# Gathering rows for the second step during the first, and computing root steps on GpSimd, in a two-layer graph kernel

## The chip, the cores and the metric

The kernel runs on one core of a Trainium2 chip. Times are device microseconds of one execution. The engines are called by the profile's names: PE (TensorE matmul; PEld its weight load), DVE (VectorE), ACT (ScalarE), POOL (GpSimd) and SP (SyncE, which here only issues DMAs). Each engine works through its own instruction queue in order. "SPq" and "POOLq" are rows for DMAs issued on SP and POOL.

## The reference, cut to what matters

There are N = 2708 nodes with D = 256 features. `adj` has about 0.3% nonzeros and a full diagonal.

```
# layer 0
x = LN(x + relu(concat(x, adj @ x) @ weight + bias))
# layer 1: X = x
R = (adj + I) / rowsum(adj + I)
Xf = X; Xa = X; Z = 0
for n in 0, 1:
    A  = top_p_attention(Xa, W1, W2, W3)   # softmax of (N, N) logits, cut at mass 0.9, renormalized
    Xf = R @ Xf
    Xa = A @ Xa
    Z += Xf @ U1[n].T + Xa @ U2[n].T
out = LN(X + Z)                            # (h - mean) / sqrt(var + 1e-5)
```

As R is sparse, R @ Xf is computed on gathered rows: for each block of 128 rows at most 7 x 128 columns of `adj` hold a nonzero outside the block's own columns.

## The kernel before, in words

The nodes form 22 row blocks of 128 (NB = 22); the last one (EDGE) has 20 rows. The order of the instructions on every engine is the order in which the program issues them.

**Layer 0** takes the time up to about 280 us: the product adj @ x (line 257), the layer norm. In the meantime POOL and DVE find the columns that each block needs (class with `take` and `end`, up to line 348). `end` (lines 324 to 348) is a chain: DVE counts, POOL writes and reads the list through DRAM with DMAs, DVE turns the counts into positions (line 339), and seven more DMAs of POOL follow. It is issued for a first part of the blocks before step 1 and for the rest at block 8 of step 1, slot 2.

**Step 1** (the loop at line 896) is the first attention, one row block after the other, in six slots g = 0 to 5 for each block (NG = 6). A slot holds transposes of the weights (line 527, copied by ACT in line 530), products (line 564), logits of a later block, and DVE's search for the cut, which has one 3 us operation for each block (line 635). Beside this, in dictionary `at`, POOL's `adj_gather(m)` (lines 360 to 371) collects the adjacency of block m: SP loads the own columns (line 364), POOL turns the names of the block before into row numbers (`name_y`, line 358), gathers 7 groups of columns with an indirect DMA each (line 367), and adds the identity to the own columns (line 369, which waits for SP's load). Four and five slots later SP stores the result to DRAM (`adj_store`, lines 373 to 381). At the end of each block SP also stores za (line 703), the running sum Z, from a tile of two buffers that DVE fills in line 702. `step1_out` returns the three steps that follow a block; the last three run after the loop.

After the loop eleven calls of `ya_pair` (line 662) project the attention result, two row blocks at a time, into the tile ya (22 blocks of 256 columns), copied from PSUM by ACT in line 675. Until then ya is not in use.

**The R product** runs in units, one matmul (line 749) for each gathered column group of a block and one for its own block: 8 units a block, 22 blocks, two passes (s = 0 and 1), 352 units. Pass 0 multiplies rows of yf_d (X U1[1]), whose result is added to v_d; pass 1 multiplies v_d. `r_load(s, m)` (line 729) issues the loads of a block as the block before it begins: the adjacency (448 KB and 64 KB, by SP), seven indirect DMAs of POOL which gather 128 rows of 1 KB each (`y_load`, line 719) into one of two buffers yg, and the own rows (line 735, SP). The first two gathers of pass 0 are issued in step 1, at block 20, slots 2 and 5 (`y_at`).

**Step 2** (the loop at line 1271) is the second attention, in 24 periods of six slots. Period `per` transposes and multiplies row block per - 2, computes logits and exponentials of block per + 2 and steps the search of the blocks between; DVE's mask (line 1087) ends each period, and 22 of them lie in the trace. `r_units(n)` spreads the R units over the slots. By period, the numbers of units are:

| period | 0, 1 | 2 to 9 | 10 | 11 to 21 |
|---|---|---|---|---|
| units each | 8 | 18 | 0 | 16 |

16 units (`first`) are computed ahead of period 0. The first 22 blocks (176 units) are pass 0, whose last unit lies in period 9; pass 1 lies in periods 11 to 21.

**The finals.** When both products of a block have arrived (`arrive`, line 785, one addition on DVE), the block takes two layer norms (with `x1b` between them), in `final_slot(i)`, called in each slot i: slot 2 loads x1b, slot 3 takes statistics on DVE, slot 5 takes `roots` (line 1216: ACT's Sqrt of the variances of up to four blocks), slot 0 of the next period takes `over` (line 1219: DVE's reciprocal and the negated mean over the root) and applies the norms (ACT's line 1191, then POOL's lines 1206 and 1207), and slot 1 stores. ACT's Sqrt and its Exp (line 844) lie in different function tables, and changing takes an ACT_TABLE_LOAD. After the loop a tail (line 1323 on) finishes the last blocks with three more root steps, one after the other.

Of the kernel before, what the change touches and what calls it, by code (L numbers as in the profile page):

```python
# [9 lines left out]
FP = mybir.dt.float32  # L10
I32 = mybir.dt.int32
AF = mybir.ActivationFunctionType
ALU = mybir.AluOpType
# [24 lines left out]
KS = 7  # L38
CAP = 160
ML = 16  # L40
CW, CC = 128, 7


# [8 lines left out]
@with_exitstack  # L52
def gnn_two_layer_kernel(ctx: ExitStack, tc: tile.TileContext, N, xT_d, x_d, adj_d, w0_d, b0_d,
                         w1_d, w2_d, w3_d, u1_d, u2_d, g_d, b_d, out_d):

    nc = tc.nc
    D = x_d.shape[1]
    DA = w1_d.shape[1]  # L80
    NB = (N + P - 1) // P
    DC = D // P
    assert N % 2 == 0 and NB % 2 == 0 and N * 2.0 ** -15 < 0.09 and DC == 2 and DA == 64
    assert SEG * (NS - 1) + 8 <= N <= SEG * NS == SEG2 * NS2 and N >= SEG2 * (NS2 - 1) + 8
    assert NB == 3 * KS + 1 and CW == P and CAP % 8 == 0 and N < NB * P
# [20 lines left out]
    c.v_d = dram.tile([P, NB, D], FP, name="v_d")  # L106
    c.own_d = dram.tile([NB, P, P], FP, name="own_d")
# [41 lines left out]
def fast_path(ctx, tc, c, flags, fint, xT_d, x_d, w0_d, b0_d, w1_d, w2_d, w3_d, u1_d, u2_d, g_d, b_d):  # L149
# [561 lines left out]
    arrived, loads, held = {}, {}, {}  # L711
    later = [[], []]
    ready = []

    def y_load(s, m):
        y = yg[:, m % 2]
        rows_d = (c.yf_d, c.v_d)[s].rearrange("p k d -> (p k) d")
        for i in range(CC):
            nc.gpsimd.indirect_dma_start(out=y[:CW, i, :], out_offset=None, in_=rows_d,  # L719
                                         in_offset=bass.IndirectOffsetOnAxis(ap=ix[:CW, m, i:i + 1], axis=0))  # L720
        y_in[s, m] = y

    def a_load(m):
# [39 lines left out]
    def za_load(m):  # L763


        if loads.get(m):
            loads[m] = 2
            return None
        loads[m] = 1
        base = work.tile([P, D], FP, tag="in", name="base", bufs=3)  # L770
        nc.sync.dma_start(out=base[:rows(m)], in_=za_d[m * P:m * P + rows(m), :])
        return base

    def r_out(s, m, acc, base):
        p = rows(m)
        if s == 0:
            nc.vector.scalar_tensor_tensor(base[:p], acc[:p, :D], rinv[:p, m:m + 1], base[:p],
                                           op0=ALU.mult, op1=ALU.add)
            nc.sync.dma_start(out=c.v_d[:p, m, :], in_=base[:p])
            if m == NB - 1:  # L780
                r_load(1, 0)
        else:
            arrive(m, base, acc, rinv[:p, m:m + 1])

    def arrive(m, base, part, scale):

        p = rows(m)
        if base is None:
            h = base = held.pop(m)
        else:  # L790
            h = work.tile([P, D], FP, tag="h", name="h", bufs=5)
# [98 lines left out]

    at = {(m // 2, 3 * (m % 2) + 1): m for m in range(4)}
    at.update({(m - 2, 3): m for m in range(4, NB)})
    y_at = {(NB - 2, 2): 0, (NB - 2, 5): 1}
    stores = []
    blocks = {}
    for t in range(NB):
# [6 lines left out]
        for g in range(NG):  # L903
# [23 lines left out]
            if (t, g) in at:  # L927
                adj_gather(at[t, g])
                stores += [(NG * t + g + i, at[t, g], i - 4) for i in (4, 5)]
            if (t, g) in y_at:  # L930
                name_y()
                y_load(0, y_at[t, g])
            if (t, g) == (NB - 1, 2):
                a_load(0)
        if t == EDGE:
# [4 lines left out]
    assert not stores and not staged and not to_turn  # L940
    r_load(0, 0)
    for f in ends:
        ya_pair()
# [219 lines left out]
    sds = small.tile([P, 8], FP, tag="sds", name="sds", bufs=1)  # L1163
    nbs = small.tile([P, 8], FP, tag="nbs", name="nbs", bufs=1)
    nc.gpsimd.memset(mvs, 1.0)

    class Final:

# [45 lines left out]
            nc.sync.dma_start(out=out_d[t * P:t * P + p, :], in_=self.h[:p])  # L1214

    def roots(a, b):
        nc.scalar.activation(sds[:, a:b], mvs[:, a:b, 1], AF.Sqrt, bias=c.eps, scale=1.0)

    def over(a, b):
        nc.vector.reciprocal(sds[:, a:b], sds[:, a:b])  # L1220
        nc.vector.scalar_tensor_tensor(nbs[:, a:b], mvs[:, a:b, 0], -1.0, sds[:, a:b], op0=ALU.mult, op1=ALU.mult)

    def final_slot(i):


        if i == 2:
            while ready and len(new) < 2:
                new.append(Final(*ready.pop(0)))
                new[-1].load()
        if i == 1:  # L1230
            while done:
                done.pop().store()
        n = len(new) + len(finals)
        if i == 3:
            for k, f in enumerate(new + finals):
                f.stats(k)
        if i == 5 and n:
            roots(0, n)
        if i == 0 and n:
            over(0, n)  # L1240
            for f in finals:
                f.end()
            for f in new:
                f.middle()
            done[:] = finals
            finals[:] = new
            new.clear()

    accs = {}


    each = NB * (CC + 1)
    first = 2 * (CC + 1)
    units = {0: CC + 1, 1: CC + 1}
    rest = each - first - sum(units.values())
    units.update({p: rest * (p - 1) // 8 - rest * (p - 2) // 8 for p in range(2, 10)})
    units.update({p: each * (p - 10) // 11 - each * (p - 11) // 11 for p in range(11, 22)})
    assert first + sum(units.values()) == 2 * each


# [10 lines left out]
    for per in range(NB + 2):  # L1271
        if per == NB + 1:
            tail.append(True)
        n_r = units.get(per, 0)
        b_act = blocks.get(per + 1)
        t_mul = per - 2 if per > 1 else None
        if t_mul is not None:
# [3 lines left out]
            b_exp = blocks[per + 2] = Block(per + 2)  # L1281
        vector = vector_slots(blocks.get(per), blocks.get(per - 1), begin_search(b_exp) if b_exp else None)
        for g in range(NG):
            n = n_r * (g + 1) // NG - n_r * g // NG
            now = later.pop(0)
            later.append([])
            if g == 0:
# [23 lines left out]
                    try_act(b_act, k, part)  # L1311
            next(vector)
            if g == 0:
                final_slot(0)
                if t_mul:
                    t = t_mul - 1
                    base = za_load(t)
                    later[0].append(lambda t=t, base=base: arrive(t, base, accs.pop(t), ras.pop(t)[:rows(t)]))
            for f in now:
                f()  # L1320
            if g and (per < NB + 1 or g < NG - 1):
                final_slot(g)
    t = EDGE
    base = za_load(t)
    last = Final(t, None)
    last.load()
    for f in later[0] + later[1]:
# [18 lines left out]
    arrive(t, base, accs.pop(t), ras.pop(t)[:rows(t)])  # L1346
    _, last.h = ready.pop()
    n = len(new) + len(finals)
    last.stats(n)
# [380 lines left out]
```

## Time and profile before

| quantity | us |
|---|---|
| median of 3 runs | 1323.01 |
| their range | 1322.98 to 1323.81 |
| profiled execution, its time | 1323.33 |
| its span in the trace | 1321.6 |
| PE busy in the span | 1237.4 |
| DVE busy | 1002.0 |
| ACT busy | 753.3 |
| POOL busy | 634.7 |
| layer 0 and preparation | up to 348 |
| step 1 | 348 to 730 |
| projections `ya_pair` | 730 to 754 |
| step 2 | 754 to 1321.6 |

The profiled execution is one of the runs, and its time stands 1.7 us above its span in the trace. Busy time counts instructions, not the gaps between them, nor register, semaphore and DMA-issuing instructions. In the group lines of a profile a row reads: line, engine, operation, output<-input, count | busy us, mean ns of one | idle time of the engine just before them, and what ended most of it. In a windows view each row is a stretch A:B, its length, the busy time of each engine with its number of instructions, the granted PE clock (1.00 is full), the busy share of the DMA engines and GB/s. In a timeline a row is start, duration, engine, line, operation, and in brackets the idle time before it with its releaser. In a waits view a row is the waiting instruction, what released it, and us in total, times, longest.

### The profile page before, as it was taken

What the parts mean: (1) busy time and instruction counts of PE and PEld (TensorE: products, weight loads), DVE (VectorE), ACT (ScalarE), POOL (GpSimd) and SP (SyncE); (2) the same over time, 40 slices, a digit from 0 to 9 for tenths busy, and PEclk for the clock granted to TensorE, in tenths of its full rate; (3) what the DMA queues carried; (4) which work ended last, traced back from release to release, by engine and by line L of the source; (5) the groups of instructions that cost most, each with busy time, mean ns of one, the idle gap of its engine ahead of it and who ended that gap; (6) DMA issues with size and microseconds to landing.
All of it is one profiled execution on the core that took longest, in us unless ns stands there. A gap on an engine that the chain in (4) does not pass through costs nothing.

```text
span 1321.6 us, 18910 instructions
## 1 busy us (share of the span) xinstructions
PE 1237.4 (94%) x5764; PEld 894.5 (68%) x5764; DVE 1002.0 (76%) x3420; ACT 753.3 (57%) x1338; POOL 634.7 (48%) x594
## 2 busy tenths in 40 slices
PE   8999999979899999999999969999999989998985
PEld 6877877833477777777775647777756766666763
DVE  2545555865999998877751399898897999899996
ACT  2010111025465556566564498878888899989931
POOL 1000000005275532677554187887847767787850
PEclk9999999989899999999998979999999999999998
DMA  7455544523222210223232155556545445544541
GB/s 191 163 173 168 167 153 142 171 67 123 92 77 82 70 62 10 76 91 99 76 77 86 55 172 179 177 178 184 172 118 159 148 128 166 173 148 146 166 108 38
DMA packets 101994, 166.28 MB, mean 126 GB/s; under 512 B 17394, under 2 KB 74358, under 8 KB 101882
## 3 DMA queue, kind: packets, MB, share of 16 engines
q1 hardware_dynamic: 75596, 108.91, 25.4%
q0 software_dynamic: 20544, 51.17, 14.1%
q10 hardware_dynamic: 5742, 4.89, 1.3%
q8 instruction: 48, 0.79, 0.2%
q14 instruction: 64, 0.52, 0.1%
HBM read 130.87 MB, written 34.03 MB: 125 GB/s over the span
## 4 chain that ended last, share of the span: by engine, by line
PE 70%; ACT 15%; DVE 11%; issue 3%; DMA 0%; ACTq 0%; DVEq 0%
PE acc L564 23%; PE acc L257 16%; PE lg L507 8%; PE tr L527 6%; PE misc L749 5%; ACT e L965 4%; ACT e L844 3%; ACT e L968 2%; DVE e L1087 2%; PE acc L651 2%; PE acc L462 2%; PE misc L426 2%; PE misc L392 2%; ACT e L848 2%; PE acc L672 2%
## 5 line engine op out<-in xcount | busy, mean ns | idle before, releaser
L530 ACT COPY wT<-tr 128x512 f32<-128x512 f32 (+2 forms) x258 | 131.8, 518 | 217.6 <-PE tr L527 215.9
L564 PE MATMUL acc<-ya,wT 128*128 128x256 f32 (+1 forms) x924 | 234.9, 394 | 11.4 <-ACT wT L530 11.0
L564 PE MATMUL acc<-x,wT 128*128 128x256 f32 (+1 forms) x924 | 230.5, 388 | 0.0
L719 POOL DMA_INDIRECT yg<-v_d,ix x154 | 195.0, 1266 | 64.6 <-issue 25.1
L564 PEld LDWEIGHTS acc<-ya,wT 128*128 128x128 f32 (+1 forms) x924 | 171.4, 194 | 66.0 <-issue 23.1
L719 POOL DMA_INDIRECT yg<-yf_d,ix x154 | 190.7, 1238 | 48.3 <-issue 24.3
L564 PEld LDWEIGHTS acc<-x,wT 128*128 128x128 f32 (+1 forms) x924 | 165.2, 189 | 71.0 <-issue 37.3
L257 PE MATMUL acc<-y,adj_t 128*128 128x257 f32 (+1 forms) x924 | 208.4, 381 | 0.0
L257 PEld LDWEIGHTS acc<-y,adj_t 128*128 128x128 f32 (+1 forms) x924 | 171.8, 189 | 32.7 <-issue 8.9
L367 POOL DMA_INDIRECT adj_t<-in_adj,ix x154 | 165.6, 1076 | 51.8 <-issue 41.7
L749 PE MATMUL misc<-yg,adj_t 128*128 128x256 f32 (+1 forms) x704 | 180.6, 392 | 5.9 <-DMA yg<-yf_d,ix 4.3
L507 PE MATMUL lg<-k,q 64*128 64x512 f32 (+3 forms) x528 | 152.4, 605 | 29.7 <-ACT e L848 22.3
L749 PEld LDWEIGHTS misc<-yg,adj_t 128*128 128x128 f32 (+1 forms) x704 | 125.2, 190 | 54.3 <-issue 23.1
L527 PE MATMUL tr<-ident,e 128*128 128x128 f32 (+2 forms) x946 | 147.9, 275 | 2.5 <-DVE e L1087 2.5
L527 PEld LDWEIGHTS tr<-ident,e 128*128 128x128 f32 (+2 forms) x946 | 114.1, 140 | 41.9 <-issue 18.8
L334 POOL DMA_DIRECT2D part_d<-e x1 | 0.6, 573 | 285.3 <-DVE e L333 285.3
L439 ACT COPY x1T<-tr 128x256 f32<-128x256 f32 (+1 forms) x22 | 8.0, 364 | 186.7 <-PE tr L438 186.7
L965 ACT ACTIVATE e<-e,st 128x2708 f32<-128x2708 f32 (+1 forms) x43 | 113.5, 2640 | 0.1
L968 ACT ACTIVATE e<-e,st 128x2708 f32<-128x2708 f32 (+1 forms) x42 | 111.0, 2642 | 0.1
L570 DVE MAX8 cand<-e 128x8 f32<-128x170 f32 (+1 forms) x352 | 87.2, 317 | 27.4 <-ACT e L514 27.4
L1029 DVE MAX8 cand<-w 128x8 f32<-128x136 f32 (+1 forms) x440 | 106.1, 285 | 0.0
L507 PEld LDWEIGHTS lg<-k,q 64*128 64x128 f32 (+1 forms) x528 | 39.5, 184 | 63.5 <-ACT e L848 30.1
(239 smaller groups left out, 1780.8 us busy)
## 6 DMA issues: line engine op xcount, KB each, us to landing
adj_t<-in_adj SPq DMA_DIRECT2D x44, 704.0 KB
adj_t<-adjc_d SPq DMA_DIRECT2D x44, 448.0 KB
adjc_d<-adj_t SPq DMA_DIRECT2D x22, 256.0 KB
base<-za_d SPq DMA_DIRECT2D x41, 128.0 KB
adjc_d<-adj_t SPq DMA_DIRECT2D x22, 192.0 KB
xt<-in_x ACTq DMA_DIRECT2D x21, 128.0 KB
x_d<-x SPq DMA_DIRECT2D x21, 128.0 KB
x1b_d<-xb SPq DMA_DIRECT2D x21, 128.0 KB
```

The lines of the kernel that those rows point to most:

```text
L257: nc.tensor.matmul(acc[:p, :n], lhsT=halves[k // KH][:kw, k % KH, :p], rhs=y[:kw, k, :n], start=k == 0, stop=stop and k == NB - 1)
L367: nc.gpsimd.indirect_dma_start(out=a[:CW, i, :], out_offset=None, in_=adj_rows, in_offset=bass.IndirectOffsetOnAxis(ap=ix[:CW, m, i:i + 1] ...
L507: nc.tensor.matmul(lg[:p, h, :b - a], lhsT=q[o, t * P:t * P + p], rhs=keys[s][o, i, :b - a], start=True, stop=True)
L527: nc.tensor.transpose(tr[:kw, k % 4, :p], e[:p, k * P:k * P + kw], ident[:p, :p])
L530: nc.scalar.copy(wT[:, :full, :p], tr[:, :full, :p])
L564: nc.tensor.matmul(acc[:p, :D], lhsT=wT[:kw, k % 4, :p], rhs=y[:kw, k, :], start=k == 0, stop=k == NB - 1)
L570: nc.vector.max(dst[:p, i * 8:(i + 1) * 8], src[:p, i * step:i * step + w])
L719: nc.gpsimd.indirect_dma_start(out=y[:CW, i, :], out_offset=None, in_=rows_d, in_offset=bass.IndirectOffsetOnAxis(ap=ix[:CW, m, i:i + 1], ...
L749: nc.tensor.matmul(acc[:p, :D], lhsT=a[:kw, k, :p], rhs=y[:kw, k, :], start=k == 0, stop=k == CC)
L965: nc.scalar.activation(scr[:b.p, :N], e, AF.Relu, bias=b.nz, scale=b.l[k], accum_out=b.relu)
L968: nc.scalar.activation(scr[:b.p, :N], e, AF.Sign, bias=b.nz, scale=b.l[k], accum_out=b.sign)
L1029: nc.vector.max(b.cand[:p, 8 * i:8 * i + 8], low[:p, SEG2 * i:SEG2 * (i + 1)])
```

## The change

1. In step 1, `y_at` now has 14 entries (NY = 14). At slot 0 of blocks 2, 3, 5, 6, 7, 8, 10, 11, 12, 14, 15, 16, 17 and 19 POOL gathers the y rows of row blocks 0 to 13 into a third of the tile ya (blocks of 7 columns, m modulo 3), and seven slots later SP stores them to a new DRAM tile yg_d (896 KB each). In step 2, `y_load(0, m)` of these 14 blocks is one SP load of 896 KB in place of seven indirect DMAs of POOL. The first two of these loads are issued at the last block of step 1, slots 0 and 3. The other eight blocks of pass 0, and all of pass 1, are gathered in step 2 as before.
2. The R units are spread in another way:

| period | 0, 1 | 2 to 8 | 9 | 10 to 21 |
|---|---|---|---|---|
| units each | 24 | 16 | 8, in slots 3 to 5 | 14 |

Pass 0 now ends with period 8, and pass 1 begins in period 9.

3. `roots` is two operations of POOL, an addition of epsilon and a power of -0.5 (by a tile that holds -0.5), so that `over` no longer takes a reciprocal. In `final_slot`, statistics and roots lie in slot 5, `over` and the norms in slot 2 of the next period, stores and loads in slot 3. The tail uses the same `roots`. Slot 5 of the last period takes statistics too, but no roots.
4. `arrive` finds its base tile in a dictionary (bookkeeping).

In the issue order of the changed program POOL has 304 rows for 248, ACT 25 fewer, DVE 16 fewer, SP 26 more and PE 3 more. On SP, the store of stage 13 stands behind the first half of the adjacency store of block 21. The ACT copy of the fourth `ya_pair` (columns 6 and 7 of ya) waits for that store.

```diff
+    def y_gather(s, m, y):
         rows_d = (c.yf_d, c.v_d)[s].rearrange("p k d -> (p k) d")
         for i in range(CC):
             nc.gpsimd.indirect_dma_start(out=y[:CW, i, :], out_offset=None, in_=rows_d,
                                          in_offset=bass.IndirectOffsetOnAxis(ap=ix[:CW, m, i:i + 1], axis=0))
+    def y_stage(m):
+        k = CC * (m % 3)
+        return ya[:, k:k + CC, :]
+    def y_store(m):
+        nc.sync.dma_start(out=c.yg_d[m], in_=y_stage(m)[:CW].rearrange("p c d -> p (c d)"))
+    def y_load(s, m):
+        y = yg[:, m % 2]
+        if s == 0 and m < NY:
+            nc.sync.dma_start(out=y[:CW, :CC, :].rearrange("p c d -> p (c d)"), in_=c.yg_d[m])
+        else:
+            y_gather(s, m, y)
         y_in[s, m] = y
...
-    y_at = {(NB - 2, 2): 0, (NB - 2, 5): 1}
+    y_at = {(2 + m + (2 * m + 3) // 7, 0): m for m in range(NY)}
+    y_stores = []
...
+            if y_stores and y_stores[0][0] <= NG * t + g:
+                y_store(y_stores.pop(0)[1])
             if (t, g) in y_at:
-                name_y()
-                y_load(0, y_at[t, g])
+                y_gather(0, y_at[t, g], y_stage(y_at[t, g]))
+                y_stores.append((NG * t + g + 7, y_at[t, g]))
+            if t == EDGE and g in (0, 3):
+                y_load(0, g // 3)
...
+    name_y()
...
     def roots(a, b):
-        nc.scalar.activation(sds[:, a:b], mvs[:, a:b, 1], AF.Sqrt, bias=c.eps, scale=1.0)
+        nc.gpsimd.tensor_scalar(sds[:, a:b], mvs[:, a:b, 1], LN_EPS, None, op0=ALU.add)
+        nc.gpsimd.tensor_tensor(sds[:, a:b], sds[:, a:b], power[:, a:b], op=ALU.pow)
     def over(a, b):
-        nc.vector.reciprocal(sds[:, a:b], sds[:, a:b])
...
     def final_slot(i):
-        if i == 2:
-            while ready and len(new) < 2:
-                new.append(Final(*ready.pop(0)))
-                new[-1].load()
-        if i == 1:
-            while done:
-                done.pop().store()
         n = len(new) + len(finals)
-        if i == 3:
-            for k, f in enumerate(new + finals):
-                f.stats(k)
-        if i == 5 and n:
-            roots(0, n)
-        if i == 0 and n:
+        if i == 2 and n:
             over(0, n)
...
+        if i == 3:
+            while done:
+                done.pop().store()
+            while ready and len(new) < 2:
+                new.append(Final(*ready.pop(0)))
+                new[-1].load()
+        if i == 5:
+            for k, f in enumerate(new + finals):
+                f.stats(k)
+            if n and not tail:
+                roots(0, n)
...
-    units = {0: CC + 1, 1: CC + 1}
+    units = {0: 3 * (CC + 1), 1: 3 * (CC + 1)}
...
-    units.update({p: rest * (p - 1) // 8 - rest * (p - 2) // 8 for p in range(2, 10)})
-    units.update({p: each * (p - 10) // 11 - each * (p - 11) // 11 for p in range(11, 22)})
+    units.update({p: rest * (p - 1) // 7 - rest * (p - 2) // 7 for p in range(2, 9)})
+    TURN = 9
+    units[TURN] = CC + 1
+    rest = each - units[TURN]
+    units.update({p: rest * (p - TURN) // 12 - rest * (p - TURN - 1) // 12 for p in range(TURN + 1, 22)})
+    def r_share(per, g):
+        late = NG // 2 if per == TURN else 0
+        upto = [units.get(per, 0) * max(0, i - late) // (NG - late) for i in (g, g + 1)]
+        return upto[1] - upto[0]
...
             if g == 0:
-                final_slot(0)
...
-            if g and (per < NB + 1 or g < NG - 1):
+            if g:
                 final_slot(g)
```

More of the change, by code (lines that the diff above doesn't have):

```diff
@@ L40 @@
 ML = 16
+NY = 14
 CW, CC = 128, 7
@@ L106, in gnn_two_layer_kernel @@
     c.v_d = dram.tile([P, NB, D], FP, name="v_d")
+    c.yg_d = dram.tile([NY, CW, CC * D], FP, name="yg_d")
     c.own_d = dram.tile([NB, P, P], FP, name="own_d")
@@ L710, in fast_path @@
     r_in, a_in, y_in = {}, {}, {}
-    arrived, loads, held = {}, {}, {}
+    arrived, loads, held, bases = {}, {}, {}, {}
     later = [[], []]
     ready = []
-    def y_load(s, m):
-        y = yg[:, m % 2]
+    def y_gather(s, m, y):
         rows_d = (c.yf_d, c.v_d)[s].rearrange("p k d -> (p k) d")
@@ L769, in za_load @@
         loads[m] = 1
-        base = work.tile([P, D], FP, tag="in", name="base", bufs=3)
+        bases[m] = base = work.tile([P, D], FP, tag="in", name="base", bufs=3)
         nc.sync.dma_start(out=base[:rows(m)], in_=za_d[m * P:m * P + rows(m), :])
@@ L782, in r_out, with arrive @@
         else:
-            arrive(m, base, acc, rinv[:p, m:m + 1])
-    def arrive(m, base, part, scale):
+            arrive(m, acc, rinv[:p, m:m + 1])
+    def arrive(m, part, scale):
         p = rows(m)
-        if base is None:
+        if m in held:
             h = base = held.pop(m)
         else:
+            base = bases.pop(m)
             h = work.tile([P, D], FP, tag="h", name="h", bufs=5)
@@ L939, in fast_path @@
         ra = ra_next
-    assert not stores and not staged and not to_turn
+    name_y()
+    assert not stores and not staged and not y_stores
     r_load(0, 0)
@@ L1165, in fast_path @@
     nc.gpsimd.memset(mvs, 1.0)
+    power = small.tile([P, 8], FP, tag="power", name="power", bufs=1)
+    nc.gpsimd.memset(power, -0.5)
     class Final:
@@ L1273, in fast_path @@
             tail.append(True)
-        n_r = units.get(per, 0)
         b_act = blocks.get(per + 1)
@@ L1283, in fast_path @@
         for g in range(NG):
-            n = n_r * (g + 1) // NG - n_r * g // NG
+            n = r_share(per, g)
             now = later.pop(0)
@@ L1313, in fast_path @@
             if g == 0:
-                final_slot(0)
                 if t_mul:
                     t = t_mul - 1
-                    base = za_load(t)
-                    later[0].append(lambda t=t, base=base: arrive(t, base, accs.pop(t), ras.pop(t)[:rows(t)]))
+                    za_load(t)
+                    later[0].append(lambda t=t: arrive(t, accs.pop(t), ras.pop(t)[:rows(t)]))
             for f in now:
                 f()
-            if g and (per < NB + 1 or g < NG - 1):
+            if g:
                 final_slot(g)
     t = EDGE
-    base = za_load(t)
+    za_load(t)
     last = Final(t, None)
@@ L1345, in fast_path @@
     accs[t] = edge_sum(accs[t], D)
-    arrive(t, base, accs.pop(t), ras.pop(t)[:rows(t)])
+    arrive(t, accs.pop(t), ras.pop(t)[:rows(t)])
     _, last.h = ready.pop()
```

## The prediction

> **What bounds the kernel now.** First the page: busy shares, then its costliest groups.
>
> ```profile
> PE 1237.4 (94%) x5764; PEld 894.5 (68%) x5764; DVE 1002.0 (76%) x3420; ACT 753.3 (57%) x1338; POOL 634.7 (48%) x594
> ...
> L719 POOL DMA_INDIRECT yg<-v_d,ix x154 | 195.0, 1266 | 64.6 <-issue 25.1
> ...
> L719 POOL DMA_INDIRECT yg<-yf_d,ix x154 | 190.7, 1238 | 48.3 <-issue 24.3
> ...
> L367 POOL DMA_INDIRECT adj_t<-in_adj,ix x154 | 165.6, 1076 | 51.8 <-issue 41.7
> ```
>
> PE is 94% busy, yet a mean hides stages. So the second view is busy time by windows, cut at starts of the mask instruction (line 1087), which ends each period of step 2.
>
> ```profile
> core 0: us, PE busy (x) PEld busy (x) DVE busy (x) ACT busy (x) POOL busy (x), PEclk, DMA share, GB/s
> 348.00:730.00 382.00, 377.02 (x1917) 270.97 (x1916) 291.11 (x1071) 224.51 (x438) 214.03 (x215) 0.99 0.24 74
> 754.00:790.20 36.20, 26.02 (x87) 16.40 (x84) 31.65 (x109) 33.91 (x50) 27.82 (x24) 0.81 0.52 155
> 807.62:952.62 145.00, 143.12 (x685) 107.89 (x684) 126.55 (x458) 119.53 (x199) 116.75 (x93) 1.00 0.60 184
> ...
> 1025.46:1048.75 23.29, 22.97 (x111) 17.16 (x110) 22.04 (x81) 19.91 (x34) 17.53 (x15) 1.00 0.54 170
> 1101.09:1207.67 106.58, 96.30 (x442) 69.17 (x441) 96.97 (x345) 99.39 (x161) 84.17 (x73) 0.98 0.51 158
> ```
>
> Step 1 (348 to 730) is PE's: 377 of 382 us, 17.5 us a block, with POOL at 214. The start of step 2 (754 to 790) is nobody's: PE waits for gathered rows. Periods 3 to 8 (807 to 952, 24.17 each) are PE's again, with 18 R units each; period 12, with 16 units, takes 23.29. In the four periods from 1101 to 1208 (26.65 each) PE, DVE, ACT leave gaps. There POOL's busy number misleads: its indirect DMAs have a gap of 0.30 between them that isn't counted. Its groups in that window are 57 gathers (73.6 busy) and 16 tensor operations (11.6), with 22.6 of gaps before them: that is the whole 106.6. Its only real wait is 5.3, for ACT's line 1191. So POOL is all but full there.
>
> The third view is POOL's timeline at the end of step 1, the fourth its waits from 345 to 715.
>
> ```profile
> 694.26 1.05 POOL L719 DMA_INDIRECT yg<-yf_d,ix  x1 [0.27 <-issue]
> 695.62 3.45 POOL L719 DMA_INDIRECT yg<-yf_d,ix  x1 [0.31 <-issue]
> 699.37 0.95 POOL L719 DMA_INDIRECT yg<-yf_d,ix  x1 [0.30 <-issue]
> ...
> 713.13 0.94 POOL L719 DMA_INDIRECT yg<-yf_d,ix  x1 [0.30 <-issue]
> ```
> ```profile
> POOL adj_t L369 <- DMA adj_t<-in_adj: 72.3, 11, 19.8
> ...
> POOL part_d L334 <- DVE yg L333: 14.2, 1, 14.2
> ...
> POOL ix L358 <- DMA adj_t<-in_adj,ix: 7.5, 6, 1.3
> ```
>
> A gather costs POOL 0.95 + 0.30 = 1.25, seven 8.75; one that meets the 3 us DVE operation (line 635 in step 1, lines 1022 and 1087 in step 2) takes 3.45 (1.6 to 2.7 more, about 2.1 on the mean). POOL ends step 1 at 714.1.
>
> The last view is ACT's timeline in one of the 26.65 periods: two table loads of 1.28, for one root of 0.30.
>
> ```profile
> 1131.09 1.28 ACT L1217 ACT_TABLE_LOAD   x1
> 1132.39 0.30 ACT L1217 ACTIVATE sds<-mvs,eps 128x4 f32<-128x4 f32 x1
> ...
> 1134.80 1.28 ACT L844 ACT_TABLE_LOAD   x1
> ```
>
> **The change part by part.** The sum is made against the profiled execution, 1323.33 (its span is 1321.6); the median, 1323.01, lies 0.3 lower, which I neglect.
>
> *1. Fourteen gathers in step 1 instead of two.* They hide only as long as POOL keeps up. POOL's end: 714.1; twelve more gathers, 12 x 8.75 = +105; their stalls, one of 2.1 in each 17.5 us, 12% = +12.6. Against this the waits that go when POOL runs behind its inputs: line 369's 72.3 less its first, 19.8, which stays = -52.5; the list's wait for DVE, -14.2; the wait for names, 7.5 and some of its neighbours, -10. Sum 755. POOL thus becomes the bound of step 1. Who waits: the y stages lie in ya. On SP, the store of stage 13 stands behind the first half of block 21's adjacency store, which needs 4 of that block's 7 columns (POOL at about 750, landing 3.0 later by the yg rows); the 917 KB store takes 3 to 5, so it lands near 756.5. It frees columns 7 to 13 of ya, and the fourth projection pair (its ACT copy stands at 736.30) writes columns 6 and 7. Behind that copy in ACT's order lie the other copies and the exponentials of the first searches. That is 20 late; as PE has by then run ahead into its other accumulators, 2 of it come back: **+18** (15 to 25; 0 if the waits that go are larger than I think). POOL also reaches the list chain (29 us long) later, so DVE's line 339, which waited 4.9 for it, holds DVE and then PE longer, and SP's late stores hold the za buffers (line 702); both are inside the 18, since PE only reaches the same wait later. The added traffic of step 1, 0.92 MB gathered and 0.92 stored for each of 14 blocks, meets DMA engines 24% busy: nothing, unless it is what stretches the store.
>
> *2. The start of step 2.* Before period 2 there are now 64 units where there were 32 (16 first, then 24 and 24 for 8 and 8). A unit is 0.433 of PE, so +13.9 to 26.0 busy in a stretch of 36.2: at least 3.7 more. But six more blocks than the two preloaded are loaded meanwhile, each 917 KB of y, 131 of own rows, 458 + 65 of adjacency and 131 to 262 of base, 1.7 to 1.8 MB. Two 704 KB loads at the kernel's start took 5.8 us (249 GB/s); the DMA share beside its rate in step 2 (184 GB/s at 0.60) allows some 300. So 6 to 7 us a block, and the next load begins only when the block before it begins. First units at 754.7 (old clock): block 2 is ready at 763.5 (POOL had it at 769.6), five more at 6.3 each: block 7 at 795; 8 units and the transposes behind it: 799.7 where the first transpose of period 2 was at 790.2. **+9.5** (2 to 14). The trace of before has no single 896 KB load; a page prices one. The Trainium skill, "DMA: Bandwidth & Descriptors" (Anatomy of one DMA), fits a GpSimd-issued DMA as 2.0 us plus bytes over 436 GB/s, an estimate of 4.1 for the y rows alone; the start would then cost about 4 instead of 9.5, and the total would be 5 lower. These loads stand on SP and share the engines with a second MB, and no row here shows over 300, so I go by the rows.
>
> *3. Fewer units in later periods.* Periods 2 to 8: 16 for 18, 24.17 to 23.30 as period 12 shows, 7 x 0.87 = **-6.1**. Period 9, the turn to the second pass, 8 units late in the period: -0.7. Period 10 (23.69, now with 14 units), 11 (24.97) and 13 (25.69), which carried 16 units and the first finals: -0.4, -1.6, -1.0. Periods 20 and 21, DVE's: -0.3. The turn adds no wait by the old rows: the last v_d store (986.6) and the first gathers (988.7) lay two us apart, and three slots now lie between them and their units. If DVE (22.0 of period 12's 23.3, 21.1 of 24.2 before it) stops them at 23.8, the 6.1 is 2.6.
>
> *4. The finals (14 to 19).* POOL loses 2 of 16 units, 1.75 gathers at 1.49 with gap and stall, 2.6; it gains two small operations (0.26 is its 128x7 tensor_scalar, 0.47 its 128x128 add; with gaps 0.6 to 1.0). So 26.65 to about 24.9. DVE, busy 24.2, loses a reciprocal of 0.16: floor 24.1. ACT, 24.8, loses 2 x 1.28 + 0.30 and falls to 21.9; PE falls to 23.2. I take 25.0: 6 x 1.65 = **-9.9** (24.2 to 26.0: -14.7 to -3.9). The pow's time is in no row. Four elements a partition lie nearest to the 0.26 row; the other end, a blocked gather's 3.45, stays in the range. `over` on DVE now waits for POOL, whose queue holds up to seven gathers ahead of the roots; three slots (12 us) lie between, 8.75 + 2 x 2.1 = 13 at worst. Behind `over` stand DVE's next search steps, so a miss would cost 1 to 2 a period: the upper end. The other moved steps cost nothing: the x1 load at slot 3 has five slots before line 1206 reads it, and the stats at slot 5 are the same eight DVE instructions. For the table load the trace and the skill differ: in "ScalarE: Activation LUTs" (What ACT_TABLE_LOAD costs) a switch is 1.28 for the load and about 1.38 of drain. The rows have 1.28, and the next instruction 0.02 behind. By the page ACT would gain 5.6 a period, by the rows 2.9; as POOL and DVE set the period after either, the sum is the same.
>
> *5. The tail.* Three root steps in a chain with nothing beside them: 0.30 on ACT and 0.16 for the reciprocal become two POOL operations and two hand-overs, 0.8 to 0.9: **+1.2** (0 to 10 with the 3.45 end).
>
> Net: 18 + 9.5 + 1.2 - 6.1 - 0.7 - 3.0 - 0.3 - 9.9 = +8.7, from 1323.3 to **1332**. The first two terms are the least sure.
>
> **The rivals.** (a) POOL keeps up, so step 1 costs nothing: the other gains hold, 1323.3 + 9.5 + 1.2 - 20 = 1314, and 1305 if the start of step 2 hides too. It decides from POOL's end of step 1: below about 736 there is no wait; my sum is 19 above. For it: POOL is 56% busy in step 1. Against it: the sum of its own rows. 0.20. (b) POOL late, but the finals don't move, because DVE waits for the pow or POOL stays full: the 9.9 goes, 1341. For it: POOL's full finals. 0.2. (c) Gains and costs cancel: 1320.4 to 1325.7, with POOL some 9 us less late. 0.12. (d) The change does not do what it says (the stores and loads wait for the same rows, the units stay bound by them): 1323 too, and counted in (c).
>
> **How the numbers follow.** My forecast (1326 to 1338) has 0.48, (b) and beyond 0.2, (a) 0.2, (c) 0.12. Faster by over 0.2% (below 1320.4; about what a measurement here can tell from no change) 0.21, within 0.11, slower 0.68. The range 1312 to 1343 takes in (a) with the start paid, and (b); the forecast's own part of it is 1326 to 1338.
>
> **What would show it.** Right: POOL without gaps in step 1, its last gather near 755; ACT's fourth ya copy released by the store of stage 13 near 755; first R matmul near 772; periods 3 to 8 at 23.3; finals near 25, no table loads there. Wrong: POOL's last step 1 gather before 740; or a pow of several us; or R units at the start waiting less than 4 us for y.

## The result and the profile after

The change made the kernel slower: 1342.37 us median (1340.56 to 1346.99, 4 runs) against 1323.41 (1322.98 to 1323.9, 4 runs), a ratio of 1.0148 with a 95% interval of 1.0122 to 1.0175. The time lies at the upper end of the stated range, but the change is 19.0, 2.2 times the forecast 8.7. The profiled execution took 1340.56, with a span of 1338.6: 17.0 above the one before.

Some experiments (called "disturbed" below) ran beside a kernel before that itself took 1366 to 1391, with engines idle for up to 41 us in step 1 on nothing that the profile shows; of these a total is used only against the kernel before beside it, and otherwise single stages of step 2.

First the page after. POOL's busy share is the same as before; only where it works has moved (98 gathers into ya, 56 instead of 154 into yg from yf_d).

```profile
PE 1238.9 (93%) x5764; PEld 894.5 (67%) x5764; DVE 994.3 (74%) x3408; ACT 730.1 (55%) x1309; POOL 639.2 (48%) x627
...
L720 POOL DMA_INDIRECT yg<-yf_d,ix x56 | 67.7, 1209 | 117.7 <-PE misc L764 99.0
...
L720 POOL DMA_INDIRECT ya<-yf_d,ix x98 | 99.4, 1014 | 27.8 <-issue 27.2
```

Then the windows, cut at the same places of the work (first R matmul, then ends of periods):

```profile
348.00:743.00 395.00, 380.99 (x1913) 273.11 (x1911) 290.71 (x1071) 224.46 (x437) 292.02 (x291) 0.97 0.40 125
...
835.43:975.26 139.83, 137.94 (x660) 101.54 (x659) 126.51 (x457) 119.58 (x199) 67.71 (x56) 1.00 0.53 156
1045.66:1070.42 24.76, 22.66 (x108) 16.29 (x106) 22.43 (x84) 21.40 (x37) 20.63 (x20) 1.00 0.54 162
1120.43:1221.96 101.53, 90.64 (x426) 65.18 (x424) 92.83 (x336) 86.69 (x147) 81.74 (x72) 1.00 0.48 147
1269.94:1296.88 26.94, 23.07 (x102) 16.08 (x102) 22.70 (x78) 5.74 (x15) 17.39 (x16) 0.94 0.43 107
```

Step 1 (here up to 743) is 13 longer, with 4.0 more of PE busy: PE waits now. Six periods of 16 units take 139.83 where 18 units took 145.00. The four periods from 1120 take 101.53 for 106.58. But the last row, period 21, which took 23.4, takes 26.94, and period 12 (1045.66 on), which took 23.3 without a final in it, takes 24.76.

Reading the starts of all 22 masks (DVE's instruction at the end of each period) of both traces gives the whole difference; here as differences of lengths:

| stretch | before | after | difference | forecast |
|---|---|---|---|---|
| up to the first R matmul | 754.7 | 773.6 | +18.9 | +18 |
| from there to mask 2 | 52.9 | 61.8 | +8.9 | +9.5 |
| periods 3 to 9 | 169.2 | 162.9 | -6.3 | -6.8 (with period 2) |
| periods 10 to 13 | 97.6 | 97.3 | -0.3 | -3.0 |
| periods 14 to 19 | 159.8 | 151.0 | -8.8 | -9.9 |
| periods 20, 21 | 46.8 | 50.2 | +3.4 | -0.3 |
| period 22 and the tail | 40.5 | 41.7 | +1.2 | +1.2 |

### The profile page after: what moved, and what is told of

It is laid out like the page before. It is cut to its first block, busy times and chain, and to the rows that moved or that the text cites. A ratio compares the mean times of both kernels' runs of the same rounds, so it can differ in the third digit from the quotient of the medians.

```text
span 1338.6 us, 18854 instructions
## 1 busy us (share of the span) xinstructions
PE 1238.9 (93%) x5764; PEld 894.5 (67%) x5764; DVE 994.3 (74%) x3408; ACT 730.1 (55%) x1309; POOL 639.2 (48%) x627
## 5 line engine op out<-in xcount | busy, mean ns | idle before, releaser
L720 POOL DMA_INDIRECT yg<-v_d,ix x154 | 190.4, 1236 | 74.0 <-DMA v_d<-base 28.5
L369 POOL DMA_INDIRECT adj_t<-in_adj,ix x154 | 175.8, 1142 | 50.7 <-issue 44.0
L764 PEld LDWEIGHTS misc<-yg,adj_t 128*128 128x128 f32 (+1 forms) x704 | 122.9, 187 | 61.9 <-issue 25.5
L720 POOL DMA_INDIRECT yg<-yf_d,ix x56 | 67.7, 1209 | 117.7 <-PE misc L764 99.0
L720 POOL DMA_INDIRECT ya<-yf_d,ix x98 | 99.4, 1014 | 27.8 <-issue 27.2
```

The costliest lines, as they stand in the source:

```text
L369: nc.gpsimd.indirect_dma_start(out=a[:CW, i, :], out_offset=None, in_=adj_rows, in_offset=bass.IndirectOffsetOnAxis(ap=ix[:CW, m, i:i + 1] ...
L764: nc.tensor.matmul(acc[:p, :D], lhsT=a[:kw, k, :p], rhs=y[:kw, k, :], start=k == 0, stop=k == CC)
```

## The experiments

Numbers of lines in these fences are those of the kernel in question (the changed kernel's are up to 24 higher than those of before). "R0" is the start of the first R matmul.

**Fewer gathers in step 1.**

```diff
-NY = 14
+NY = 8
-    y_at = {(2 + m + (2 * m + 3) // 7, 0): m for m in range(NY)}
+    y_at = {(4 + 2 * m, 0): m for m in range(NY)}
```

> The change with 8 row blocks gathered in step 1 instead of 14 (NY = 8, at blocks 4, 6, ..., 18), all else as changed. Theory (POOL is the bound of step 1 and that costs the first 18.9 us): POOL has 6 x 8.75 = 52 us less to do and ends step 1 before 728, so the first R matmul is back near 755, and the time falls by about 18 to 1324 (1320 to 1327). Rival (the delay comes from traffic, or from the stores' place on SP, with any number of gathers): at least half of the delay stays, 1333 or more.

1324.34, a ratio of 1.000 (0.9991 to 1.001) to before. R0 is at 755.5, and every later stretch is as in the change, to 0.3 us: 18.1 of the 18.9 of step 1, and nothing else, goes. POOL's last step 1 operation ended at 727, and the 59.2 us that DVE's line 704 waits for stores of za in the change (first row of waits below) are gone; it waits for PE instead. The theory holds: with 14 gathers step 1 is late, with 8 it is not. As fewer gathers also mean fewer stores and less traffic, this run alone doesn't part the three.

**Which way POOL's lateness reaches PE.** In the change DVE waits in line 704 for a za buffer; the store that frees it stands on SP behind adjacency stores that wait for POOL. The waits of DVE and POOL in step 1 after:

```profile
DVE za L704 <- DMA za_d<-za: 59.2, 6, 20.2
```
```profile
POOL adj_t L371 <- DMA adj_t<-in_adj: 16.3, 1, 16.3
POOL ix L360 <- DMA adj_t<-in_adj,ix: 10.6, 4, 3.4
```

At the end, ACT's fourth copy into ya waits for the last y store, which SP issues only at 750.32, behind the adjacency store of block 21 (ACT's timeline, then SP's, of the change):

```profile
747.46 0.59 ACT L677 COPY ya<-acc 128x512 f32<-128x512 f32 x1 [0.78 <-PE acc L674]
...
756.22 0.59 ACT L677 COPY ya<-acc 128x512 f32<-128x512 f32 x1 [8.08 <-DMA yg_d<-ya]
```
```profile
749.82 0.33 SPq L379 DMA_DIRECT2D adjc_d<-adj_t  x1
750.32 0.32 SPq L728 DMA_DIRECT2D yg_d<-ya  x1
```

So the adjacency stores are issued six slots later and the y stores five, and with that the last y store comes to stand ahead of block 21's; nothing is left out:

```diff
-                stores += [(NG * t + g + i, at[t, g], i - 4) for i in (4, 5)]
+                stores += [(NG * t + g + i + (6 if t > 1 else 0), at[t, g], i - 4) for i in (4, 5)]
-                y_stores.append((NG * t + g + 7, y_at[t, g]))
+                y_stores.append((NG * t + g + 12, y_at[t, g]))
```

> The change with SP's adjacency and y stores of step 1 issued later, the same kernel as in the run before of this name. Theory (POOL's own queue is the bound of step 1): DVE does not wait for za behind SP, PE leaves step 1 near 730, but the last y store still makes the projections wait; first R matmul at 766 to 774. Rival (SP's order makes the delay): first R matmul at 755 to 760, and the time is 13 to 18 below the change's.

R0 came to 762.2, between the two forecasts; the time was 1334.06 (two runs; ratio to before 1.0081, 1.0061 to 1.0101). Both theories hold a part. POOL itself ends 2 earlier only (its last addition at 748.89 instead of 750.98); yet the waits for stores of za are gone, and the ya copy comes at 746.48:

```profile
746.48 0.59 ACT L677 COPY ya<-acc 128x512 f32<-128x512 f32 x1 [5.07 <-DMA yg_d<-ya]
```
```profile
741.67 0.32 SPq L728 DMA_DIRECT2D yg_d<-ya  x1
742.09 0.38 SPq L733 DMA_DIRECT2D yg<-yg_d  x1
752.19 0.32 SPq L379 DMA_DIRECT2D adjc_d<-adj_t  x1
```

The store leaves 8.65 earlier. So 11.4 of the 18.9 at R0 are SP's order; all the traffic is still there. The other 7.5 fit POOL's queue: the copy still waits 5.07 for the last y store, and that store is issued 2.0 after POOL's last gather into ya, which ends at 739.65. Of the 11.4 some come back: the adjacency of block 0 now stands behind block 21's stores, the time from R0 to mask 1 is 33.8 instead of 30.4, and 7.9 stay at mask 1. By the end of the span 5.5 stay: period 10 is 0.6 longer and the time behind the last mask 1.8, for reasons not looked for. An earlier run of the same kernel was disturbed (1513, R0 at 930) and says nothing on this.

> The change with SP's stores of step 1 issued later: the adjacency stores 10 and 11 slots after their gathers instead of 4 and 5 (the first four blocks as before), the y stores after 12 slots instead of 7. Nothing is left out. Theory (POOL's own queue is the bound of step 1): DVE no longer waits for za behind SP and PE leaves step 1 near 730 instead of 742, but the projections then wait longer for the last y store; the first R matmul comes at 766 to 774, the time is 1334 to 1343. Rival (SP's order makes the delay, POOL itself would be in time): first R matmul at 755 to 760, time 1324 to 1329.

**The start of step 2.** Here the y loads of blocks 2 to 7 are left out, and their units multiply whatever rows lie in the buffers.

```diff
-        if s == 0 and m < NY:
+        if s == 0 and 2 <= m < 8:
+            pass
+        elif s == 0 and m < NY:
```

> The same kernel as in the run before of this name: the change with the y loads of blocks 2 to 7 left out. Theory (these loads set the start): period 2 begins its mask 4 to 6 us earlier than in the change, 1336 to 1338. Rival (DVE's results hold the PSUM tiles of the R units, and the loads are beside that): at most 2 us earlier, 1340 to 1343.

From R0 to mask 2 took 58.1, where the change took 61.8 and the late-store kernel beside it 61.9 (both disturbed, the total is 1516; an earlier run of the same kernel, also disturbed, gave 58.9 and 1506). So the loads are worth 3.0 to 3.8 of the 8.9, less than the theory's 4 to 6 and more than the rival's 2: neither is it alone. In the change PE's wait for these rows is

```profile
PE misc L764 <- DMA yg<-yg_d: 4.0, 2, 3.1
```

PE's waits without the loads name the next limit:

```profile
PE misc L766 <- DVE base L794: 6.8, 3, 4.3
```

DVE's addition of an R result is what frees the PSUM tile of the R units. And PE has more work: busy 41.25 of 52.90 from R0 to mask 2 before, 51.48 of 61.83 after. How the rest of the 8.9 divides between these two is not shown. The earlier run's expectation was:

> The change with the y loads of blocks 2 to 7 left out, so those units multiply rows that lie in the buffers from before. Theory (the loads of 6 to 7 us a block set the start of step 2): period 2 ends 4 to 6 us earlier, as only PE's 13.9 us more work is left, and the time is 1336 to 1338. Rival (the start is held by DVE's results and PE's order, not by the loads): period 2 as in the change within 1 us, 1341 to 1343.

**The finals: who sets 26.65?** Three kernels: the roots on GpSimd alone (the third part on the kernel before), the change without that part, and the kernel before with the root left out.

```diff
-        nc.scalar.activation(sds[:, a:b], mvs[:, a:b, 1], AF.Sqrt, bias=c.eps, scale=1.0)
+        nc.scalar.activation(sds[:, a:b], mvs[:, a:b, 1], AF.Identity, bias=c.eps, scale=1.0)
```

> The kernel before with the third part of the change alone: roots on GpSimd, steps three slots apart. Theory (in the finals POOL is full, so ACT's table loads cost little): the seven periods stay at 26 to 27 each, the tail costs 1 to 2, the time is 1321 to 1326. Rival (ACT with its two table loads sets these periods): they fall to about 24.8, 1311 to 1314.

> The change without its third part: 14 blocks gathered in step 1 and the new distribution of units, but roots by ACT's Sqrt, with the table loads, in the old slots. Theory (POOL sets the finals, and 14 units instead of 16 relieve it): periods 12 to 19 at 25 to 25.5, time 1341 to 1346. Rival (ACT sets them): they stay at 26.6, eight of them, and the time is 1355 to 1358.

> The kernel before with the root left out: ACT computes variance + epsilon by Identity in place of Sqrt, the same instruction of 0.30 us in the same place without a change of tables. All 15 table loads of the finals go (19 us of ACT). Theory (POOL full in the finals): 26.65 falls by at most 0.5 a period, 1318 to 1323. Rival (ACT sets the finals): 24 to 25 a period, 1307 to 1312.

Roots on GpSimd alone: 1334.0, slower than before (1.007, 1.0047 to 1.0092), outside both forecasts. The change without them: 1348.36 (1.0196, 1.017 to 1.0221), between. Root left out: 1315.0 (0.9936, 0.9918 to 0.9955), between, 3 from each; by its periods it is near the rival. Its total still holds 2.0 that have nothing to do with the finals' periods: from the last mask to the end it took 26.76 for 24.79, at a granted clock of 0.69 against 0.92 up to the last computing instruction, with PE's line 550 at 5.74 for 3.30. Windows over four periods of finals in each (roots alone; without them; root left out):

```profile
1099.06:1208.47 109.41, 97.59 (x446) 67.65 (x444) 93.12 (x341) 87.58 (x149) 88.39 (x81) 1.00 0.51 154
```
```profile
1127.27:1232.89 105.62, 93.92 (x426) 66.98 (x425) 94.41 (x340) 98.44 (x159) 69.84 (x64) 0.97 0.46 142
```
```profile
1097.51:1198.52 101.01, 95.17 (x442) 67.88 (x441) 94.86 (x345) 88.38 (x153) 83.89 (x73) 1.00 0.54 167
```

The third row refutes the theory that POOL is full and ACT's table loads cost little: POOL has the same gathers as before, and the period falls from 26.65 to 25.25. What went is POOL's one real wait, which the prediction saw and counted as part of a full POOL (before, in the same four periods as the prediction's row):

```profile
POOL yg L1206 <- ACT yg L1191: 5.3, 4, 1.3
```

With the root left out POOL doesn't wait for ACT at all in these periods, and they are 5.6 shorter. The clock (0.98 before, 1.00 here) explains little of that: PE's busy time differs by 1.1. The second refutes it from the other side: POOL has 14 units' gathers and is busy 69.84 of 105.62, and the period stays at 26.2 to 26.7. The first suggests that POOL was nonetheless near its end: with the roots on top of 16 units a period takes 27.3, and PE waits for gathered rows (3.4 us in these four periods).

**Roots by Ln and Exp on ACT.** If one table held both, the loads would go without GpSimd.

```diff
-        nc.scalar.activation(sds[:, a:b], mvs[:, a:b, 1], AF.Sqrt, bias=c.eps, scale=1.0)
+        nc.scalar.activation(sds[:, a:b], mvs[:, a:b, 1], AF.Ln, bias=c.eps, scale=1.0)
+        nc.scalar.activation(sds[:, a:b], sds[:, a:b], AF.Exp, scale=-0.5)
...
-        nc.vector.reciprocal(sds[:, a:b], sds[:, a:b])
```

> The kernel before with the root as Ln and Exp on ACT, once more. Theory: periods 13 to 19 at 24.2 and 25.2 to 25.3, all else as before: 1313 to 1318. Rival: 1321 or more, the gain being lost elsewhere.

1318.39 (0.9961, 0.9947 to 0.9975): between, and the reason was another. The trace has 31 table loads, 13 more than before, and yet periods 14 to 18 take 25.19. ACT's timeline in one of them:

```profile
1128.38 1.28 ACT L1217 ACT_TABLE_LOAD   x1
1129.67 0.30 ACT L1217 ACTIVATE sds<-mvs,eps 128x4 f32<-128x4 f32 x1
1129.99 1.28 ACT L1218 ACT_TABLE_LOAD   x1
1131.28 0.21 ACT L1218 ACTIVATE sds<-sds 128x4 f32<-128x4 f32 x1
1131.43 0.58 ACT L530 COPY wT<-tr 128x512 f32<-128x512 f32 x1
1131.91 1.12 ACT L844 ACTIVATE e<-lg,nmax 128x1024 f32<-128x1024 f32 x1
```

Both loads lie ahead of the copy of line 530. With the root left out, ACT sat idle there for 2.93, waiting for PE's transposes:

```profile
1154.50 0.59 ACT L530 COPY wT<-tr 128x512 f32<-128x512 f32 x1 [2.93 <-PE tr L527]
```

Two loads (2.57) fit in that gap. Before, one lay in it, and the other behind the copy, ahead of line 844's Exp, on the chain that runs from that copy through ACT to the end of the period; this is the theory that the next run tests. Two earlier runs, both disturbed, gave 25.2 to 25.3 in periods 14 to 19, totals of 1369.03 and 1379.69, and ratios of 0.9961 (0.9935 to 0.9988) and 0.9967 (0.9942 to 0.9992).

> The kernel before with the root as ACT's Ln and then Exp with scale -0.5 (two instructions for the Sqrt, and DVE's reciprocal goes). Theory (the finals are a loop of ACT and PE in which one table load of 1.28 lies): if Ln and Exp share a table, the loads of the finals go and each of the seven periods falls from 26.65 to 25.3 plus 0.2 to 0.3 for the second instruction; 1315 to 1318. Rival: the compiler loads tables for Ln and Exp too, and the time is 1323 or more.

> The kernel before with the root as Ln and Exp on ACT, once more. Theory: the seven periods from 13 to 19 fall to 24.2 to 25.3, all else as before; 1313 to 1318. Rival: 1321 to 1324, as the gain is lost in other periods.

To test the place alone, the kernel before keeps its Sqrt, and one Exp of a single column that nobody reads pulls the second load forward:

```diff
         nc.scalar.activation(sds[:, a:b], mvs[:, a:b, 1], AF.Sqrt, bias=c.eps, scale=1.0)
+        if not tail:
+            nc.scalar.activation(warm, c.eps, AF.Exp)
```

> The kernel before with one instruction more after each Sqrt outside the tail: ACT's Exp of one column into a tile that nobody reads, so that the table load back to Exp lies there, and not before line 844's Exp. Same number of table loads. Theory (of the two loads only the one before line 844 lies in the loop of ACT and PE; the other, and this one, lie where ACT waits for PE's transposes): periods 14 to 19 at 25.2 to 25.3, tail as before, 1313 to 1316. Rival (each load costs its 1.28 wherever it lies): 26.65 or more stays, 1323 to 1326.

Periods 14 to 19 take 25.19 to 25.26 (26.6 before) with both loads still there in each, and the tail 24.6. The run was disturbed, so the total (1363.34) is only to be read against before beside it, 0.9939 (0.9902 to 0.9975). Four periods of it:

```profile
1141.29:1242.28 100.99, 95.17 (x442) 67.89 (x441) 94.83 (x346) 99.81 (x165) 83.88 (x73) 1.00 0.55 167
```

ACT is busier than before (99.81 of 100.99 against 99.39 of 106.58), and the period is shorter. So the load ahead of line 844 lies on the chain that sets the period, and the other does not. Which engines close that chain is not shown: the profile's view of it passes through ACT and DVE before, and through ACT and PE with the root left out.

**What the roots on GpSimd cost.** The changed kernel in period 21 (POOL's timeline, then waits of DVE and of ACT):

```profile
1284.67 0.95 POOL L720 DMA_INDIRECT yg<-v_d,ix  x1 [0.30 <-issue]
1285.92 0.94 POOL L720 DMA_INDIRECT yg<-v_d,ix  x1 [0.30 <-issue]
1286.90 0.26 POOL L1241 TENSOR_SCALAR sds<-mvs 128x3 f32<-128x3 f32 x1
1287.25 0.89 POOL L1242 TENSOR_TENSOR sds<-sds,power 128x3 f32<-128x3 f32 x1
```
```profile
DVE nbs L1245 <- POOL sds L1242: 2.4, 1, 2.4
DVE bst L1205 <- POOL yg L1231: 1.5, 2, 0.8
```
```profile
ACT yg L1215 <- DVE nbs L1245: 9.0, 1, 9.0
```

The roots stand behind seven gathers, one of them held by a DVE operation; `over` on DVE waits 2.4, and behind it all of DVE's search. The second row is the statistics, now in slot 5, which wait 1.5 for POOL's line 1231. DVE is busy for 22.70 of the 26.94, and with these 3.9 that is nearly the whole period. Two kernels do without the roots on GpSimd and have the steps of the finals in their old slots: the change with the root left out on ACT (Identity, as above), and eight gathers with Ln and Exp.

> The change without roots on GpSimd, and with the root left out: ACT's Identity in place of Sqrt, in the old slots, so neither table loads nor POOL waits. Theory: first R matmul at 773.8 and start as in the change; periods 12 to 19 at 24.8 each without the longer ones, period 21 at 23; time 1334 to 1338. Rival (the long periods 16, 17 and 21 come from the gathers alone): they stay, 1340 or more.

> Eight row blocks gathered in step 1, the new distribution of units, and the root by Ln and Exp on ACT in the old slots instead of GpSimd. Theory (roots on GpSimd cost period 21 some 3.6 and periods 16 and 17 some 2.5, because they stand behind seven gathers): those waits go, periods 12 to 19 take 24.8 to 25.1, period 21 23.4, and the time is 1316 to 1320. Rival (these waits have another cause, such as the early finals): 1323 to 1326, as with the roots on GpSimd.

Both were disturbed (1496.9 and 1443.48 beside 1373.79 for the kernel before; R0 at 910 and 858), so the totals tell nothing. In the stretches that they share with the change, period 21 took 22.55 and 21.95 instead of 26.95, and periods 16 and 17 25.25 and 24.76, and 25.20 and 24.70, instead of 25.54 and 26.99. Period 21 in the first of them is DVE's alone, without a wait:

```profile
1418.02:1440.56 22.54, 19.63 (x86) 13.80 (x87) 22.30 (x77) 5.96 (x16) 14.85 (x12) 0.92 0.49 112
```

The change with ACT's Sqrt (above, not disturbed) also took 22.55 there. That these waits come from the gathers alone is refuted: all three kernels have the gathers of pass 1. Against the first the roots on GpSimd, with the slots moved for them, cost 4.4 in period 21, and 2.0 in periods 16 to 18 together (76.8 against 74.8), of which 1.0 is left over periods 14 to 19 (151.0 against 150.0).

**A version that beats both.** Eight gathers, Ln and Exp, and 16 units in periods 0 to 9 and 11 to 21:

```diff
-    units = {0: 3 * (CC + 1), 1: 3 * (CC + 1)}
+    units = {0: 2 * (CC + 1), 1: 2 * (CC + 1)}
...
+    units.update({p: rest * (p - 1) // 8 - rest * (p - 2) // 8 for p in range(2, 10)})
+    units.update({p: each * (p - 10) // 11 - each * (p - 11) // 11 for p in range(11, 22)})
```

> Eight blocks gathered in step 1, root by Ln and Exp on ACT, 16 units in periods 0 to 9 and 11 to 21, as in the run before of this name. Theory: first R matmul at 755.5, 4 to 5 lost by period 2, 0.87 saved in each of periods 2 to 9, finals 25.2: 1310 to 1315. Rival (the start is full, or the finals stay at 26.65): 1319 or more.

1314.53, 0.9935 (0.9919 to 0.9952) of before and faster than the change by 28. The kernel before with Ln and Exp alone took 1318.39 beside it, so 5.0 of the gain on before (1323.36 there) come with Ln and Exp, and 3.9 with the eight gathers and the new units. From R0 to mask 2 took 56.0, 3.1 more than before; periods 4 to 9 23.3 each; finals 25.2. From the last mask to the end it takes 28.2 instead of 24.8, as Ln and Exp change tables there with little beside them: eight loads, where before had none, and DVE waits 7.2 for these roots. It is not safe, though: the same kernel, disturbed, took 1428.61, 1.029 times before beside it (1.0244 to 1.0336).

> Eight row blocks gathered in step 1, root by Ln and Exp on ACT, and 16 units in periods 0 to 9 and 11 to 21 (before: 8, 8, then 18 each). Theory: first R matmul at 755.5; the start costs half of what 24 and 24 cost, 4 to 5 by period 2; periods 2 to 9 save 0.87 each; finals 25.2; 1310 to 1315, faster than the kernel before. Rival (the start is full already, or the finals keep their 26.65): 1319 or more.

Two last kernels put Sqrt and the one-column Exp in the place of Ln and Exp, one with these units, one with the change's.

> Eight blocks gathered in step 1, 16 units in periods 0 to 9 and 11 to 21, and Sqrt followed by the one-column Exp instead of Ln and Exp, so that the tail has its single loads again. Theory: as with Ln and Exp (1314.5) but 2 to 4 less in the tail: 1310 to 1313. Rival: the tail's length has another cause, 1314 to 1316.

> The same with the change's distribution of units (24, 24, 16 in periods 2 to 8, 8, then 14) instead. Theory: the start costs 9 instead of 4, periods 9 to 11 gain 2, but the finals take 24.8 and begin a period earlier: 1312 to 1316, not better than the run beside it. Rival: fewer units in each final pay: below 1310.

They ran disturbed (1414.95 and 1435.45, 1.0307 and 1.0452 times before), so whether they beat 1314.53 is open. What can be read: from the last mask to the end 23.0 and 23.9 instead of 28.2, with DVE's wait for the roots at 0.4 in the first of them, so the longer tail was for the most part the loads; finals 25.2 to 25.3 with 16 units, 24.8 to 25.25 with 14.

## Why the prediction was less than half of what came

Two steps failed. "Periods 20 and 21, DVE's: -0.3" gave the new waits of DVE for POOL no price outside periods 14 to 19: +3.4 came. "-0.4, -1.6, -1.0" for periods 10, 11 and 13 left out that finals begin earlier: -0.3 came, with period 12, instead of -3.0. Together they are 6.4 of the 8.3 by which the profiled span missed the sum. The other terms came near in size, some of them by luck.

**Step 1 (+18 forecast, +18.9).** Size, POOL's end (755 forecast, 751.4 measured) and the wait of the fourth ya copy (landing near 756.5 forecast, copy at 756.22) were right. The step "both are inside the 18" was right as a sum but blurred the cause: 11.4 of 18.9 at R0 went when SP's order changed while POOL ended only 2 earlier.

**Start of step 2 (+9.5, +8.9).** Size right, but by luck: the loads, on which the 9.5 was built, are 3.0 to 3.8 of it. What is left has PE's added work in it, which the prediction had only as a floor of 3.7, and R results that wait for DVE, which it did not weigh; their shares are open. PE's 4.0 of waiting for y stand right at its own sign of being wrong, "less than 4 us". Two readings behind the step were off as well. The start was not "nobody's": its own row has ACT busy for 33.91 of 36.20. And "no row here shows over 300" is wrong: between 754 and 800 the rates of before reach 386 GB/s in a slice of 1.2 us.

**Periods 2 to 9 (-6.8, -6.3).** 23.30 as read from period 12. Seven times 0.87 was one too many, since period 2 lies in the start.

**Periods 10, 11 and 13 (-3.0; with period 12 -0.3).** The step that failed is "-0.4, -1.6, -1.0": it took those periods as they stood, only lighter, and period 12 as unchanged. As pass 1 begins in period 9, finals begin earlier: the first root step lies in period 11 (at 1028.6) instead of 13 (at 1053.4). Period 12, now with finals, went from 23.30 to 24.76, which is 1.5 of the 2.7; in the version that beats both, where pass 1 begins as late as before, it is 23.30 again. Periods 10, 11 and 13 each fell by less than forecast.

**Finals (-9.9, -8.8).** The number was near by luck, the reasoning wrong. "POOL is all but full there" does not hold: the rows that it adds up come to 107.8 for a stretch of 106.6, and 5.3 of them are a wait for ACT. (Its 1.49 for a gather with gap and stall is 1.58 by those rows, 0.2 a period.) The run with the root left out and the run with 14 units and Sqrt contradict that POOL sets the period. What set 26.65 was a chain through ACT with one table load in it. The pow, put near 0.26, takes 1.04 for four columns and 0.89 for three. The change's 24.76 is also that of the kernel with the root left out and 14 units, so there POOL's roots add nothing; what sets it was not tested.

**Period 21 (-0.3 for periods 20 and 21, +3.4).** The largest miss: 3.7. The prediction saw the queue ("seven gathers ahead of the roots", "13 at worst" against 12 us) and priced a miss at 1 to 2, but only as an upper end for periods 14 to 19. Period 21, which it called DVE's, so that a wait of DVE adds to it in full, was left out of the step; `over` waits 2.4 there. "The other moved steps cost nothing" failed there too: the statistics in slot 5 wait another 1.5 for POOL.

**Tail (+1.2, +1.2 with period 22).** The sum is right in part by luck: from the last mask to the end it is +2.0 (26.75 against 24.79), and period 22, for which nothing was forecast, gave back 0.7.

By terms: 0.9 - 0.6 + 0.5 + 2.7 + 1.1 + 3.7 = 8.3, which is 17.0 - 8.7. From 17.0 to 19.0 it is mostly the 1.8 by which the profiled execution, the fastest of four, stands below the median. Of the rivals, (b) came nearest in time (1341; its own sum gives 1341.9) but not in cause: the finals did gain.

## What to carry to other kernels

An engine that looks full need not be the bound: see whether a wait is counted in it, find what the period's chain passes through, and test it by taking the suspected cost out. Work moved to an idle engine is paid by whoever stands behind it in a queue: here SP's stores, za, and a root behind seven gathers. A fixed cost such as a table load is worth what its place is worth, and moving it by one small instruction may do what moving the work to another engine was meant to do.

## What the hardware showed that I had not expected

- In the changed kernel a power on GpSimd takes 1.04 us for 128x4, 0.57 at the least for one column, against about 0.26 for the addition beside it.
- Ln and then Exp took a table load each, in every root step (28 loads in 14 steps).
